# A graph layer with top-p attention on one core: work moved off GpSimd in one stage, a shorter sort on exponentials in the next

## Chip, cores and metric

The kernel runs on one core of one Trainium2 chip. The metric is device time in microseconds (us) from start to end of the program. Engines are named as in the profile: PE (TensorE matmul), PEld (its weight load), DVE (VectorE), ACT (ScalarE), POOL (GpSimd) and SP (the engine that only issues DMAs).

## What is computed

Two layers over 3327 nodes with 256 features, all in float32. The first is a graph attention layer with a gated update. The second, which holds nearly all of the change, makes two steps; in each, every node attends to all nodes, and of its probabilities only the largest that together reach 0.9 are kept:

```python
q = X @ W1.T @ W2.T
k = X @ W3.T
probs = softmax(q @ k.T)
sp, idx = probs sorted downwards, and its order
keep_sorted = cumsum(sp) - sp < 0.9
A = probs * (that mask, put back in place)
A = A / max(A.sum(-1), 1e-12)
...
for n in range(2):
    A = top_p_attention(Xa)
    Xf = R @ Xf          # R: sparse adjacency + identity, rows scaled to 1
    Xa = A @ Xa
    Z = Z + Xf @ U1[n].T + Xa @ U2[n].T
h = X + Z
x = layernorm(X + (layernorm(h) * ln_g + ln_b))
```

## The kernel before

Rows are worked on in 26 tiles of 128 (the last has 127). The program has four stages.

**Layer 0** (0 to 396 us). `Layer0.run` overlaps up to seven tiles; `Layer0.tile` is a generator in which `to(k)` puts what follows into the k-th turn, and a new tile opens every 6 turns. Its row result x1 is normalized at line 1049.

**Step 0** (396 to 1010 us). `Layer1.parts_0` defines the parts of a tile by name, and the table `ORDER_0` (line 75) gives each a tick. A tile opens every 32 ticks (`EVERY0`), so parts of up to six tiles interleave; a tick modulo 32 tells where a part stands in the steady order. PE, ACT, DVE and POOL run strictly in the order written (`manual_schedule`). A tile's path: logits for all nodes (L1720, copied by ACT at L1723), the eight largest of each 208 by MAX8 (L1736), a sort of the 40 largest by five rounds of MAX8 and MATCH_REPLACE8 (L1754, L1756), the cut-off `limit` (L1424 to L1444), signs (L1448), the list of the nodes that any row needs (L1457 to L1527), five gathers of those nodes on POOL (`needed`, L1537), their logits again (`turned` L1575, `by_nodes` L1594, `weights` L1602, `kept` L1607), the product (`attention` L1613, `one_over` L1620, `xa` L1626), and `xa_u` (L1353), whose result `c_out` copies (L1647) and `c_add` adds to x1 on POOL (L1652). Beside it runs the sparse side: five gathers of neighbours on POOL (L648), membership masks (`member`, five comparisons a tile, L1321), `adj_1`, `adj_2` (L1328, L1333), `xf` (L1338), `xf_u` (L1353), `y_out` (L1365, L1370), and the additions `y_add` and `y_add2` on POOL (L1374, L1378). `bias` adds ln_b to x1 on POOL and stores it (L1894). `limit_parts` splits the limit into three bfloat16 numbers in five small POOL operations (L1550 to L1554).

**Step 1** (1010 to 1609 us). `run` works tile by tile. For tile i the 26 transposes of the masked probabilities (`turn`, L1941, copied by ACT at L1943) and the product (`times`, L1957) go in 7 groups; in slots after the groups, parts of tiles i+1 and i+2 are put in. PE, ACT and DVE keep the order written; POOL's order is chosen by the framework. DVE's order for one tile is: 16 of tile i+1's 20 MAX8 of 167 (L1736), the last eight (L1741), a sort of 72 by nine rounds (L1754, L1756), 4 MAX8 of tile i+2 (`EARLY_GROUPS`), the cumulated sum and cut-off (`list_3`, L1832 and `settle`), and in slot 5 `mask`: MATCH_REPLACE8 over 3335 elements of the logits (L1860), then a comparison and product over 3327 (L1846), which makes the tile that PE transposes next. Logits of tile i+2 are made in slots 0, 2, 4 and 6. The exponentials of tile i+1 stand in slots 1 and 2 (L1812).

**Ends** (1609 to 1821 us). Rows whose kept set is longer than the list are put aside during step 1 and done in three groups of 128 (`hard`). Should more remain, a slow program computes everything anew.

Two logits arrays `l` and two probability arrays `p` alternate between tiles. PSUM pools hold two buffers each.

Of the kernel before, what the change touches and what calls it, by code (L numbers as in the profile page):

```python
# [79 lines left out]
        (37, "sort_2"), (40, "exp1"), (42, "adj_1"), (43, "sort_3"), (45, "exp0 exp_list"), (47, "bias"),  # L80
        (49, "settle_1 settle_2"), (58, "sign1"), (59, "sign0 adj_2"), (69, "count"), (72, "xf"), (74, "any_row"),
        (75, "prefix"), (77, "places"), (79, "hot_l hot_h"), (80, "xf_turned"), (82, "hot_b"), (83, "xf_copy"), (88, "placed"), (91, "node"), (94, "xf_u"),
        (99, "told"), (101, "y_out"), (102, "limit_parts"), (107, "y_add"), (112, "y_add2"), (116, "limit_turned"), (118, "limit_row"), (122, "index"), (124, "needed0"), (127, "needed3"), (135, "needed1"),
        (141, "needed4"), (143, "needed2"), (145, "turned"), (148, "turned_copy"), (150, "by_nodes weights"),
        (160, "kept"), (163, "attention"), (167, "one_over"), (170, "xa"), (172, "qk0"), (175, "qk1 qk2"),
        (178, "xa_u"), (180, "qk3"), (184, "c_out"), (191, "c_add"),
# [5 lines left out]
LIST = (40, 72)  # L92
EARLY_GROUPS = [
    g for h in range(2) for g in range(-(-h * HALF // GROUP[1]), (h * HALF + LC) // GROUP[1])
]
# [454 lines left out]
class Shared:  # L550


    def __init__(self, tc, ctx, x, W1T, W2T, W3T):
# [16 lines left out]
        self.weights = W1T, W2T, W3T  # L570
        self.xt_of = {}
# [123 lines left out]
class Layer0:  # L695
# [187 lines left out]
    def tile(self, t):  # L883
# [166 lines left out]
        move_rows(nc.scalar, sh.x1_rows[t * P : t * P + r, :], x1, r)  # L1050
        yield from to(42)
# [123 lines left out]
class Layer1:  # L1175
    def __init__(self, sh, ctx, U1T, U2T, ln_g, ln_b, out):
# [19 lines left out]
        self.b = keep.tile([P, D], F32, name="ln_b")  # L1196
        nc.sync.dma_start(self.b, ln_b.partition_broadcast(P))
        self.xu = keep.tile([P, NT, D], F32, name="xu")
        self.power = keep.tile([P, 1], F32, name="power")
        nc.vector.memset(self.power, -0.5)  # L1200
        self.ident16 = keep.tile([P, P], BF16, name="ident16")
# [61 lines left out]
    def parts_0(self, t):  # L1263
# [49 lines left out]
        @part  # L1313
        def bias():
            self.x_and_bias(t)

        @part
        def member():
            v.m1 = work.tile([P, EB, P], F32, tag="m", name=f"m{tag}")
            for b in range(EB):  # L1320
                nc.vector.tensor_scalar(v.m1[:, b, :], sh.col1, sh.erow[:, t, b : b + 1], None, ALU.is_equal)  # L1321
            nc.sync.dma_start(self.members[t], v.m1)
# [39 lines left out]
        @part  # L1362
        def y_out():
            v.y = work.tile([P, STEPS, D], F32, tag="xt", name=f"y{tag}", bufs=3)
            nc.scalar.activation(  # L1365
                v.y[:r].rearrange("p s d -> p (s d)"), v.py[:r], AF.Copy, scale=sh.rinv[:r, t : t + 1]
            )
            move_rows(nc.sync, sh.y_rows[t * P : t * P + r, :], v.y[:r, 1, :], r)
            v.own = work.tile([P, D], F32, tag="xf2", name=f"own{tag}")
            nc.scalar.activation(v.own[:r], v.y[:r, 1, :], AF.Copy, scale=sh.rinv[:r, t : t + 1])  # L1370

        @part
        def y_add():
            nc.gpsimd.tensor_tensor(sh.x1[:r, t, :], sh.x1[:r, t, :], v.y[:r, 0, :], ALU.add)  # L1374

        @part
        def y_add2():
            nc.gpsimd.tensor_tensor(sh.x1[:r, t, :], sh.x1[:r, t, :], v.own[:r], ALU.add)  # L1378
# [168 lines left out]
        def limit_parts():  # L1547
            v.three = self.st.tile([P, 3], BF16, tag="three", name=f"three{tag}", bufs=4)
            left = small("lleft", f"lleft{tag}")
            nc.gpsimd.tensor_copy(v.three[:r, 0:1], v.limit[:r])  # L1550
# [265 lines left out]
    def list_2(self, i):  # L1816
        for _ in self.items[i].sort:
            pass
# [637 lines left out]
```

## Time and profile before

| what | us |
|---|---|
| median of 3 runs (1827.29 to 1838.53) | 1833.26 |
| the profiled execution, its own time | 1823.47 |
| its span, first to last instruction | 1821.3 |
| layer 0 | 396.0 |
| step 0, full part (460 to 903) | 443.0 |
| step 1, steady part (1010.84 to 1491.00) | 480.2 |
| step 1, last tiles (1491 to 1609) | 118.0 |
| ends | 212.3 |

The stages were cut by the windows view at the first mask of step 1 (1010.84), and at its last regular and its last mask (1491.00 and about 1609). In a timeline line the columns are start, duration, engine, source line, operation, output and inputs with their shapes, count, and in brackets the idle time before it with what ended it. In the windows view a line is a stretch: its length, then busy time and instruction count of PE, PEld, DVE, ACT, POOL, then the granted clock of PE (1.00 is full), the share of DMA and GB/s.

### The profile page before, as it was taken

The numbers are of one execution on the slowest core, as the hardware profiler recorded it, in microseconds if no ns is written. First come the engines' busy times: TensorE is split into PE (matmuls) and PEld (weight loads), VectorE is DVE, ScalarE is ACT, GpSimd is POOL, SyncE is SP. The second block draws the span as 40 slices with busy tenths as digits, with TensorE's granted clock in tenths as the row PEclk, the third lists the DMA queues.
The fourth block names the chain that finished last, engine by engine and source line by source line (L and its number), as shares of the span: only waits on it lengthen the run. The fifth ranks groups of instructions, "written<-read, shape, count | busy, mean of one in ns | idle before, by whom it ended". The sixth has DMA issues, their size and how long they took to land.

```text
span 1821.3 us, 27585 instructions
## 1 busy us (share of the span) xinstructions
PE 1468.1 (81%) x7865; PEld 978.0 (54%) x7865; DVE 1432.0 (79%) x4680; ACT 1070.6 (59%) x2494; POOL 1156.2 (63%) x1962
## 2 busy tenths in 40 slices
PE   6399999977888888888887799999999987973333
PEld 5255555544544555545553577666667765652332
DVE  5788887448877888888841999999999996787793
ACT  3366666746766777777652456666666654666511
POOL 1577777625766777777653477777777776565311
PEclk9799999977889999999996899999999998995666
DMA  8877773323333333334332122222222212100000
GB/s 276 296 255 234 232 226 100 84 83 97 98 101 106 107 100 107 106 111 114 101 90 61 42 56 65 61 61 60 60 61 59 60 49 62 40 15 24 3 3 4
DMA packets 98686, 176.20 MB, mean 97 GB/s; under 512 B 25970, under 2 KB 61041, under 8 KB 98524
## 3 DMA queue, kind: packets, MB, share of 16 engines
q0 software_dynamic: 26480, 74.24, 16.0%
q1 hardware_dynamic: 53790, 83.24, 13.9%
q10 hardware_dynamic: 18254, 16.86, 2.8%
q8 instruction: 64, 1.05, 0.2%
q14 instruction: 98, 0.80, 0.1%
HBM read 137.17 MB, written 37.21 MB: 96 GB/s over the span
## 4 chain that ended last, share of the span: by engine, by line
PE 29%; POOL 22%; DVE 19%; ACT 15%; issue 11%; DMA 4%; POOLq 0%; ACTq 0%; SPq 0%; DVEq 0%
POOL g L648 10%; PE pav L1957 6%; DVE array L1860 5%; PE pl L1720 3%; POOL g L1537 3%; DVE array L1846 2%; DMA g<-x1k,uidx 2%; DVE p L1846 2%; ACT at L1943 2%; ACT array L1812 2%; PE pc L1353 2%; ACT p L1812 2%; PE pt L1941 2%; PE pav L1613 2%; PE pavh L1957 2%
## 5 line engine op out<-in xcount | busy, mean ns | idle before, releaser
L1957 PE MATMUL pav<-xu,at 128*128 128x256 f32 (+2 forms) x1352 | 334.1, 392 | 25.3 <-ACT at L1943 25.1
L1957 PEld LDWEIGHTS pav<-xu,at 128*128 128x128 f32 (+2 forms) x1352 | 247.7, 192 | 106.8 <-ACT at L1943 46.1
L1736 DVE MAX8 cand<-array 128x8 f32<-128x167 f32 (+5 forms) x921 | 243.7, 335 | 25.2 <-ACT array L1723 25.2
L1723 ACT COPY array<-pl 128x416 f32<-128x416 f32 (+3 forms) x402 | 182.4, 505 | 131.2 <-PE pl L1720 130.6
L1720 PE MATMUL pl<-kT,qT 64*128 64x416 f32 (+3 forms) x804 | 213.7, 573 | 19.5 <-ACT array L1723 14.6
L648 POOL DMA_INDIRECT g<-whx,edge x130 | 141.8, 1090 | 46.8 <-issue 36.1
L648 POOL DMA_INDIRECT g<-y_rows,edge x130 | 137.0, 1054 | 46.3 <-issue 30.5
L648 POOL DMA_INDIRECT g<-x_rows,edge x130 | 136.1, 1047 | 43.5 <-issue 34.8
L1537 POOL DMA_INDIRECT g<-x1k,uidx x130 | 137.7, 1060 | 37.9 <-issue 34.1
L1943 ACT COPY at<-pt 128x512 f32<-128x512 f32 (+2 forms) x182 | 93.4, 542 | 114.3 <-PE pt L1941 114.2
L1720 PEld LDWEIGHTS pl<-kT,qT 64*128 64x128 f32 (+1 forms) x804 | 73.0, 190 | 95.3 <-issue 49.8
L1754 DVE MAX8 lst<-cand 128x8 f32<-128x160 f32 (+3 forms) x364 | 113.4, 311 | 8.1
L867 DVE FIND_INDEX8 at<-ones,array 128x8 uint32<-128x840 f32 (+1 forms) x104 | 105.5, 1027 | 0.0
L1860 DVE MATCH_REPLACE8 array<-gone,array 128x3335 f32<-128x3335 f32 (+1 forms) x26 | 94.0, 3617 | 0.0
L1756 DVE MATCH_REPLACE8 cand<-lst,cand 128x160 f32<-128x160 f32 (+3 forms) x312 | 92.8, 297 | 0.0
L1992 POOL TENSOR_TENSOR h<-h,xb 128x256 f32<-128x256 f32 (+1 forms) x26 | 87.5, 3364 | 2.0
L1613 PE MATMUL pav<-g,w 128*128 128x257 f32 (+1 forms) x260 | 66.7, 405 | 16.6 <-ACT y L1365 13.2
L1884 PE MATMUL pxf<-g,m 128*128 128x256 f32 (+1 forms) x260 | 68.5, 414 | 3.7 <-DVE base L2027 3.7
L1613 PEld LDWEIGHTS pav<-g,w 128*128 128x128 f32 (+1 forms) x260 | 49.5, 198 | 39.9 <-ACT y L1365 28.8
L1652 POOL TENSOR_TENSOR x<-x,c 128x256 f32<-128x256 f32 (+1 forms) x26 | 22.0, 846 | 76.7 <-ACT c L1647 76.7
L1884 PEld LDWEIGHTS pxf<-g,m 128*128 128x128 f32 (+1 forms) x260 | 50.9, 204 | 36.3 <-issue 25.2
L988 PE MATMUL acc<-g,m 128*128 128x259 f32 (+1 forms) x260 | 64.1, 393 | 6.7 <-ACT m L984 6.7
(547 smaller groups left out, 3781.0 us busy)
## 6 DMA issues: line engine op xcount, KB each, us to landing
array<-in_adj_dram SPq DMA_DIRECT2D x23, 1248.0 KB
array<-in_adj_dram SPq DMA_DIRECT2D x23, 415.5 KB
members<-m SPq DMA_DIRECT2D x26, 320.0 KB
m<-members SPq DMA_DIRECT2D x26, 320.0 KB
whx<-table ACTq DMA_DIRECT2D x25, 129.5 KB
x_rows<-x ACTq DMA_DIRECT2D x25, 128.0 KB
x1k<-x ACTq DMA_DIRECT2D x25, 128.0 KB
xb_rows<-xb SPq DMA_DIRECT2D x25, 128.0 KB
```

Source lines behind the costliest of these rows:

```text
L648: self.nc.gpsimd.indirect_dma_start(out=dst[:, b, :], out_offset=None, in_=table[:, :], in_offset=bass.IndirectOffsetOnAxis(ap=self.edge[: ...
L867: nc.vector.max_index(at[:r, g, :], self.ones8[:r], ad[:r, g, :])
L1537: nc.gpsimd.indirect_dma_start(out=v.g2[:, b, :], out_offset=None, in_=sh.x1k[:, :], in_offset=bass.IndirectOffsetOnAxis(ap=v.idx[:, b : b ...
L1613: nc.tensor.matmul(v.acc[:r, : D + 1], v.w[:, b, :r], v.g2[:, b, : D + 1], start=(b == 0), stop=(b == UB - 1))
L1720: nc.tensor.matmul(pl[:r, :w], q[on], self.sh.kT[on, n, s : s + w], start=True, stop=True)
L1723: nc.scalar.copy(l[:r, h * HALF + s : h * HALF + s + w], pl[:r, :w])
L1736: self.nc.vector.max(cand[:r, g * 8 : g * 8 + 8], src[:r, g * group : min(N, (g + 1) * group)])
L1754: nc.vector.max(lst[:r, k : k + 8], cand[:r])
L1860: nc.vector.match_replace(rev, gone[:r], rev, -BIG)
L1884: nc.tensor.matmul(acc[:r, :D], v.m[:, b, :r], v.g[:, b, :], start=(b == 0), stop=(b == EB - 1))
L1943: nc.scalar.copy(at[:, :full, :r], pt[:, :full, :r])
L1957: nc.tensor.matmul(v.acc[: v.r, :D], at[:k, j - 4 * g, : v.r], V[:k, j, :], start=(j == 0), stop=(j == NT - 1))
```

## The change

In step 0, `y_add` and `c_add` go from POOL to DVE, which reads the products from PSUM; the copies in `y_out` and `c_out` that fed POOL go away; `limit_parts` goes to ACT; ln_b is added in layer 0 instead of in `bias`; the five comparisons of `member` become one; `ORDER_0` is laid out anew. In step 1, the largest logit comes from the candidates (`highest`), the exponentials are made a tile earlier, and exponentials instead of logits are sorted: all candidates at or above a bound are summed at once, if that sum is tested to lie under the threshold, and the next 40 are sorted in five rounds. Ties and mask work on `p` alone. The slots change: the logits of tile i+2 in slots 0 to 3, their MAX8 in slots 1 to 4, `mask` of tile i+1 in slot 4 after them.

```diff
 ORDER_0, ticks (before -> after):
-  (59, "adj_2") (72, "xf") (80, "xf_turned") (101, "y_out") (107, "y_add") (112, "y_add2") (102, "limit_parts")
-  (145, "turned") (163, "attention") (170, "xa") (178, "xa_u") (184, "c_out") (191, "c_add")
+  (48, "adj_2") (60, "xf") (66, "xf_turned") (101, "y_out") (103, "y_add") (105, "limit_parts")
+  (148, "turned") (164, "attention") (173, "xa") (181, "xa_u") (187, "c_out") (190, "c_add")
-LIST = (40, 72)
+LIST = (40, 40)
...
 # Layer0.tile, after x1 is made at turn 41
+        xb = self.work.tile([P, D], F32, tag="n", name=f"xb{t}")
+        nc.gpsimd.tensor_tensor(xb[:r], x1, sh.b[:r], ALU.add)
+        move_rows(nc.sync, sh.xb_rows[t * P : t * P + r, :], xb[:r], r)
...
 # parts_0
-            for b in range(EB):
-                nc.vector.tensor_scalar(v.m1[:, b, :], sh.col1, sh.erow[:, t, b : b + 1], None, ALU.is_equal)
+            nc.vector.tensor_tensor(v.m1, sh.col1 (broadcast), sh.erow[:, t, :] (broadcast), ALU.is_equal)
-            nc.gpsimd.tensor_tensor(sh.x1[:r, t, :], sh.x1[:r, t, :], v.y[:r, 0, :], ALU.add)
-            nc.gpsimd.tensor_tensor(sh.x1[:r, t, :], sh.x1[:r, t, :], v.own[:r], ALU.add)
+            for s, scale in enumerate((sh.rinv, self.rinv2)):
+                nc.vector.scalar_tensor_tensor(
+                    x1, v.py[:r, s * D : (s + 1) * D], scale[:r, t : t + 1], x1, ALU.mult, ALU.add
+                )
-            nc.gpsimd.tensor_tensor(sh.x1[:r, t, :], sh.x1[:r, t, :], v.c[:r], ALU.add)
+            nc.vector.tensor_tensor(sh.x1[:r, t, :], sh.x1[:r, t, :], v.pc2[:r, :D], ALU.add)
...
+    def list_1(self, i):
+        nc.vector.tensor_scalar(v.thr2[:r], v.sums[:r, 0:1], v.sums[:r, 1:2], 2.0 * TOP_P, ALU.add, ALU.mult)
+        nc.vector.tensor_reduce(high[:r], self.ranks(ec, r)[:, :, SKIP], AX.X, ALU.max)
+        v.last = self.last_eights(ec, r, tag)
+        nc.vector.scalar_tensor_tensor(v.cand[:r], ec[:r], high[:r], ec[:r], ALU.is_ge, ALU.mult, accum_out=above[:r])
+        nc.vector.scalar_tensor_tensor(over[:r], above[:r], 2.0, v.thr2[:r], ALU.mult, ALU.is_ge)
+        nc.vector.scalar_tensor_tensor(top[:r], over[:r], 2.0, high[:r], ALU.mult, ALU.max)
+        nc.vector.scalar_tensor_tensor(v.cand[:r], ec[:r], top[:r], ec[:r], ALU.is_lt, ALU.mult)
+        nc.vector.scalar_tensor_tensor(v.e[:r, 0:1], over[:r], 0.5, above[:r], ALU.is_lt, ALU.mult)
+        for _ in self.sort(v.cand, r, LIST[1], tag, v.lst):
+            pass
...
 # mask
-        self.drop(v.l[:r], v.d, v.t, r, 0, tag)
+        self.drop(v.p[:r], v.d, v.t, r, 0, tag)
-            v.p[:r], v.l[:r, :N], v.t[:r], v.p[:r], ALU.is_ge, ALU.mult, accum_out=sA[:r]
+            v.p[:r], v.p[:r], v.t[:r], v.p[:r], ALU.is_ge, ALU.mult, accum_out=sA[:r]
...
 # run, step 1
+                for k, pair in enumerate(pairs):
+                    slot(k, self.some_logits, i + 2, pair)
                 if i + 1 < total:
                     self.list_1(i + 1)
-                    slot(1, self.exp, i + 1, 0)
-                    slot(1, self.list_2, i + 1)
-                    slot(2, self.exp, i + 1, 1)
-                    slot(2, self.exp_list, i + 1)
+                    slot(0, self.list_2, i + 1)
+                for k, pair in enumerate(pairs):
+                    slot(k + 1, self.largest, i + 2, pair)
                 if i + 2 < total:
-                    slot(2, self.some_eights, i + 2, EARLY_GROUPS)
+                    slot(4, self.highest, i + 2)
+                    slot(5, self.exp_candidates, i + 2)
+                    slot(5, self.exp, i + 2, 0)
+                    slot(6, self.exp, i + 2, 1)
                 if i + 1 < total:
                     slot(3, self.put_aside_2, i)
-                    slot(3, self.list_3, i + 1)
-                    slot(5, self.mask, i + 1)
+                    slot(4, self.mask, i + 1)
                     slot(6, self.put_aside_1, i + 1)
...
-                for k, pair in enumerate(pairs):
-                    slot(2 * k, self.some_logits, i + 2, pair)
```

In the new `list_2` stand the cumulated sum and `settle` of the former `list_3`, now 40 wide. `largest(i, pair)` issues the MAX8 of those groups of 167 whose columns have all been copied: four after each of the first two pairs of chunks, six after the third, six after the fourth. At the handover, `first_1` makes the MAX8 of both first tiles of step 1 instead of one, and the exponentials of both follow. The three last groups (`hard`) keep a list of 72 (`HARD_LIST`).

## The prediction

> **What bounds the kernel now.** I read the page first, then the stages in the windows view, then one regular period of each large stage in windows and timeline. The page's first lines say that no engine is full over the whole:
>
> ```profile
> PE 1468.1 (81%) x7865; PEld 978.0 (54%) x7865; DVE 1432.0 (79%) x4680; ACT 1070.6 (59%) x2494; POOL 1156.2 (63%) x1962
> ```
>
> The averages hide two loops with different limits. Windows of step 0 (length, then busy PE, PEld, DVE, ACT, POOL, then the clock), one line for a tile at reduced clock, one at full clock:
>
> ```profile
> 690.00:711.80 21.80, 19.01 (x128) 11.07 (x127) 17.55 (x70) 15.26 (x32) 15.49 (x21) 0.92 0.37 103
> 752.71:773.11 20.40, 17.55 (x127) 10.44 (x126) 17.63 (x70) 15.24 (x33) 15.53 (x21) 1.00 0.39 111
> ```
>
> Here nobody is at 100%. The once-a-tile index instruction (L1532) starts at 460.17 and 21 tiles later at 902.95: 21.1 us a tile on average. What links the tiles is in the timeline of the second window:
>
> ```profile
> 750.36 0.16 DVE L1620 TENSOR_SCALAR rA<-pav 128x1 f32<-128x1 f32 x1 [2.01 <-PE pav L1613]
> ...
> 754.88 1.00 POOL L1537 DMA_INDIRECT g<-x1k,uidx  x1 [0.31 <-issue]
> ...
> 757.82 0.30 PE L1575 MATMUL pk<-ident,g 128*64 128x128 f32 x1 [1.43 <-DMA g<-x1k,uidx]
> ...
> 763.99 0.73 POOL L1652 TENSOR_TENSOR x<-x,c 128x256 f32<-128x256 f32 x1 [1.51 <-ACT c L1647]
> ```
>
> A ring: the last gather leaves POOL at 755.88, its data reach PE at 757.82, PE and ACT make c, POOL waits 1.51 us for c, adds it, and only then issues the gathers of the next tile. POOL idles 1.5 us, PE 1.4, DVE 2.0; each waits for the other. Outside that wait POOL is occupied for 18.9 of 20.4 us, since each of ten gathers takes 1.0 plus 0.3 of issue.
>
> Step 1, one period, and the loop inside it (chunk copies and the mask):
>
> ```profile
> 1238.45:1261.42 22.97, 21.58 (x107) 16.03 (x107) 21.62 (x64) 14.40 (x34) 17.22 (x29) 1.00 0.21 60
> ```
>
> ```profile
> 1238.53 3.62 DVE L1860 MATCH_REPLACE8 array<-gone,array 128x3335 f32<-128x3335 f32 x1
> ...
> 1242.18 4.17 DVE L1846 SCALAR_TENSOR_TENSOR array<-array,t,array 128x3327 f32<-128x3327 f32 x1
> ...
> 1242.95 3.99 POOL L1992 TENSOR_TENSOR h<-h,xb 128x256 f32<-128x256 f32 x1
> ...
> 1246.50 1.06 PE L1941 MATMUL pt<-ident,array 128*128 128x128 f32 x8 [0.62 <-DVE array L1846]
> ...
> 1247.07 3.81 DVE L1736 MAX8 cand<-array 128x8 f32<-128x167 f32 x16
> ...
> 1247.81 1.99 PE L1957 MATMUL pav<-xu,at 128*128 128x256 f32 x8 [0.24 <-ACT at L1943]
> ...
> 1250.17 0.97 PE L1720 MATMUL pl<-kT,qT 64*128 64x416 f32 x4
> ...
> 1251.17 0.92 ACT L1723 COPY array<-pl 128x416 f32<-128x416 f32 x2 [0.31 <-PE pl L1720]
> ```
>
> DVE has no idle but 0.45 us for the list's exponentials; after one tile's mask it starts at once on the next tile's MAX8, all of whose logits are there. DVE is the bound, PE (21.6) close behind. Masks start at 1010.84 and, 21 tiles later, at 1491.00: 22.87 us each.
>
> [...] the POOL addition above takes 3.99 us beside the two-input L1846, where the same shape takes 0.73 (L1991) elsewhere. [...] Here a window of 4 us with 2.20 us of PE work (692 to 696) is followed by one at 0.70 of the clock, while gaps near 1 us in other tiles leave it at 1.00.
>
> **Step 0, part by part.** *POOL* loses L1374, L1378, L1652, L1894 (0.75 + 0.75 + 0.85 + 0.77, means of the groups) and the five limit operations (0.25 apart, 1.3): 4.4 us, from 18.9 to 14.5; and nothing on it waits for c any more, so the ring is open. *DVE* gains two PSUM additions for y and one for c. Nearest row: DVE L1029 and L1338, 256 wide from PSUM, 0.42 and 0.41; together 1.25. `member`: five L1321 take 1.1; [...] (an estimate; the 640-wide L1607 takes 0.95): minus 0.3. DVE without its wait is 20.4 - 2.0 = 18.4; plus 0.95 is 19.4. Bounds: 18.8 if the small operations that POOL slows (L1490 to L1493, means 0.35 to 0.61 where the shortest are 0.18) speed up, 20.5 if the new order makes DVE wait again. *ACT* loses L1370 (0.51), L1647 (0.36), half of L1365 (0.2), gains five operations of about 0.2: zero, and it is 15.3 busy of 20. *PE* has the same work, 17.6. New period 19.7, DVE's, with 0.3 for waits; 21 x (21.1 - 19.7) = 29, with the ramps **-31 us** (-13 to -48).
>
> **Layer 0.** 26 additions of 0.77 and their stores are moved here. POOL is 7.8 busy of 10 us a tile, PE 10.0 (window 337.47 to 347.50), so 0.77 fits, but POOL now waits in order for ACT's x1 (L1049) and behind it stand a later tile's gathers; on SP the stores stand between the adjacency loads. **+3 us** (0 to +10).
>
> **Step 1: work.** DVE loses four rounds of sort, start to start 0.78: 3.1; the wait for the list 0.45, a memset 0.06, about 0.3 from 40 instead of 72 columns. It gains a reduction (0.19), two operations of 160 with one accumulator read (0.33 + 0.33 + 0.08; nearest row L1756, 0.31) and four tiny ones at 0.23: 1.85. Net -2.1: 20.9 us. If that set the pace, PE's 21.6 would be next.
>
> **Step 1: order.** But it does not. On DVE, `mask` of tile i+1 now stands behind `largest` of the last chunks and `highest` of tile i+2, and those chunks are in slot 3 of tile i, behind PE work that needs the mask of tile i. From mask to mask, with the durations above:
>
> - mask end to first transpose 0.14; transposes to first product 1.31 (1246.50 to 1247.81);
> - three groups of product 1.83, transposes 0.53, chunk 0.90 (1247.81, 1249.64, 1250.17, 1251.07): 3 x 3.26 = 9.78; then 1.83 + 0.53 to the fourth chunk: 13.6 in all;
> - chunk start to first copy's end 1.5 (copies start 1.0 after it, 0.46 each); six MAX8 at 0.24, last one full, 1.5 (the second copy is hidden under the first three); reduction 0.25; the two `gone` operations 0.53;
> - MATCH_REPLACE8 with its load 3.71; L1846 3.69 alone (1014.57) to 4.17 beside POOL's addition.
>
> Sum 13.6 + 11.2 to 11.65 = **24.8 to 25.3**, 25.1. DVE waits for chunks about 4 us in it, PE for the mask: after the fourth chunk PE has only 0.9 + 1.9 + 0.3 + 2.7 + 2.4 = 8.2 us of work against 11.5, a hole of 3 us. Before, that path had slack: chunks in slot 6, MAX8 after the mask. The hole may cost clock: a first group at low clock took 3.43 instead of 1.99 (1019.71), with its transposes 1.6 more. I take a fifth of the tiles, 0.3: 25.4 (24.8 to 26.7). 21 x (25.4 - 22.87) = **+53 us** (+40 to +80).
>
> **Handover and end.** Before, 9.3 us pass from last MAX8 (1001.5) to mask. Now: six more MAX8 1.5, `highest` 0.3, candidates' exponentials 0.4, two halves 1.9 each, `list_1` 5.5, cut-off 1.6, 0.5: 13.6. **+4**. The last tiles (1491 to 1609) hold a wait of PE for POOL's flag, 10.5 us before L2005; the flag's cut-off now comes earlier: **-4** (-14 to +8). The ends are unchanged: a list of 72 as before. Loading ln_b earlier and the single `rinv2` operation: under 1 us.
>
> **Sum.** -31 + 3 + 53 + 4 - 4 = **+25**. On the profiled execution, 1823.5 + 25 = 1848.5; it lies 9.8 below the median of the runs, 1833.3, to which I add the same 25: **1858**.
>
> **Rivals.**
> - *The loop does not close*: if the fourth chunk's way to the mask is hidden (the chunk reaches DVE before DVE is through with its other work), step 1 runs at PE's 21.6 to 21.8: 21 x -1.15 = -24, total -52, about 1781. For it: DVE and PE loads are both below 22. Against: the order is written out and strict. It decides at a period of 24.2: there the loss of 21 x 1.33 equals the 28 gained elsewhere. Chance 0.20; this one ends on the other side.
> - *The clock falls in every tile*, 25.1 + 1.6 = 26.7: +80, total +52, 1885. For it: the hole of 3 us; against: [...] work around it is dense. 0.14.
> - *Step 0 gains nothing*, as three more operations on DVE's strict order wait for PE while POOL's release is worth nothing: +56, 1889. For it: DVE is the next bound by 1 us only. 0.07.
> - *The bound test does not hold*, too many rows are put aside, and the slow program runs: thousands of us. No view speaks for it; 0.01.
> - The forecast: 0.58, its own range 1832 to 1884.
>
> Faster by over 1% (below 1815): the first rival and a corner of the forecast, 0.21. Within 1% (to 1851.6), about what a measurement can tell: 0.22 of the forecast and 0.02, 0.24. Slower: 0.55. The range: 1786 leaves about 0.12 below, 1898 about 0.06 above.
>
> **What will show it.** Right: in step 1, mask starts 25 us apart, PE's first transpose waiting about 3 us for DVE L1846's successor, DVE's last MAX8 waiting for ACT, DVE busy below 21. Wrong: a wait under 1 us there and a period below 23. In step 0: a period of 19.5 to 20, no POOL wait for c, DVE's wait for L1620's successor below 0.5; wrong if the period stays at 20.4 or more. In layer 0: POOL waiting for ACT x1 before the new addition, stage end near 399. At the handover: the first mask some 13 to 14 us after the last MAX8.

## The result and the profile after

The changed kernel takes 2042.11 us (median of 4 runs, 2030.28 to 2050.05) against 1830.38 for the kernel before beside it: ratio 1.1144, 95% interval 1.1074 to 1.1213. It is slower by a ninth, where the prediction had +25 us (1858), and outside the predicted range.

The page's line of engines. Every engine but DVE and POOL has more busy time than before, PE by 143 us for the same 7865 instructions:

```profile
PE 1611.3 (79%) x7865; PEld 1054.9 (52%) x7865; DVE 1396.9 (68%) x4499; ACT 1081.6 (53%) x2569; POOL 1039.8 (51%) x1754
```

Cut at the same marks as before (the index instruction L1532 of step 0, the masks of step 1), the profiled executions (own times 1823.47 and 2050.05, spans 1821.3 and 2048.3) differ by 227.0 us:

| stage | before | after | predicted | measured |
|---|---|---|---|---|
| layer 0, to the first index instruction | 438.7 | 451.2 | +3 | +12.5 |
| step 0, 25 intervals of that instruction | 522.6 (20.90 each) | 637.8 (25.51 each) | -31 | +115.2 |
| last index instruction to first mask | 49.6 | 59.9 | +4 | +10.3 |
| step 1, 21 steady tiles | 480.2 | 573.0 | +53 | +92.8 |
| last tiles and ends | 330.2 | 326.3 | -4 | -3.9 |

Windows of the changed kernel: one regular tile of step 0, one of step 1 (length; busy PE, PEld, DVE, ACT, POOL; clock):

```profile
839.65:864.41 24.76, 20.77 (x131) 11.66 (x130) 17.05 (x69) 15.64 (x36) 10.65 (x12) 0.93 0.30 85
1366.96:1394.27 27.31, 24.06 (x107) 17.81 (x107) 19.67 (x59) 14.74 (x34) 16.55 (x28) 0.88 0.17 51
```

In step 0 DVE and POOL are busy for less than the prediction said (17.05 and 10.65), PE for more (20.77 instead of 17.6), and yet a tile takes 24.8: no engine is full, a longer chain is the bound. PE's surplus goes with its clock. The same windows over the full part of step 0, for the kernel before, the changed kernel, and the changed kernel with the old ticks (an experiment below):

```profile
460.00:903.00 443.00, 383.17 (x2641) 224.72 (x2641) 368.15 (x1448) 319.98 (x649) 324.12 (x421) 0.96 0.38 105
460.00:990.00 530.00, 437.11 (x2526) 246.64 (x2523) 341.60 (x1364) 307.01 (x677) 215.61 (x224) 0.85 0.29 80
460.00:903.00 443.00, 380.12 (x2696) 227.39 (x2693) 366.33 (x1467) 333.09 (x728) 238.17 (x238) 0.99 0.40 102
```

The clock of PE is 0.85 instead of 0.96 and 0.99, and PE is busy for about 21 us a tile instead of 18 (busy time over length, times the interval between tiles). No run takes this apart from the waits that come with it.

In step 1 DVE lost 2.0 us of work a tile and the tile became 4.3 longer; PE's work grew by 2.5 because its clock is 0.88.

Where step 0 waits, by the waits view of the stretch 460 to 990:

```profile
POOL uidx L1532 <- DMA back<-ulist: 234.6, 20, 16.7
DVE x L1650 <- ACT xu L1646: 136.6, 19, 9.5
ACT w L1602 <- PE plt L1594: 71.6, 18, 5.2
```

The wait that stood at this place before, POOL's for c (44.2 us in step 0), is gone. DVE now waits three times as long for the other half of the same product, and POOL waits for the list of nodes. The timeline of one period and of the start of the next:

```profile
864.41 0.19 POOL L1532 TENSOR_SCALAR uidx<-back 128x5 uint32<-128x5 f32 x1 [10.87 <-DMA back<-ulist]
...
871.98 1.98 PE L1357 MATMUL pc<-u,xtq 128*128 128x512 f32 x4
...
875.60 0.37 PE L1594 MATMUL plt<-qT,kg 64*128 64x128 f32 x1
...
876.55 0.27 PE L1594 MATMUL plt<-qT,kg 64*128 64x128 f32 x1 [0.57 <-issue]
...
880.33 3.78 PE L1357 MATMUL py<-u,xft 128*128 128x512 f32 x4
...
880.43 0.76 ACT L1602 ACTIVATE w<-plt 128x384 f32<-128x384 f32 x2 [5.08 <-PE plt L1594]
...
881.08 1.68 ACT L1448 ACTIVATE array<-array,limit 128x1663 bf16<-128x1663 f32 x1
...
882.65 0.37 ACT L1646 COPY xu<-pc 128x256 f32<-128x256 f32 x1
...
883.06 0.42 DVE L1650 TENSOR_TENSOR x<-x,pc 128x256 f32<-128x256 f32 x1 [7.18 <-ACT xu L1646]
...
885.38 0.81 DVE L1607 SCALAR_TENSOR_TENSOR w<-w 128x640 f32<-128x640 f32 x1
...
886.11 0.15 DVE L1524 TENSOR_TENSOR node<-node,pu 32x20 f32<-32x20 f32 x1
...
886.34 2.41 PE L1613 MATMUL pav<-g,w 128*128 128x257 f32 x10 [0.17 <-DVE node L1524]
...
889.53 0.19 POOL L1532 TENSOR_SCALAR uidx<-back 128x5 uint32<-128x5 f32 x1 [11.42 <-DMA back<-ulist]
...
902.16 0.37 PE L1594 MATMUL plt<-qT,kg 64*128 64x128 f32 x1
```

The product pc is complete at 873.96. Its copy `c_out` (L1646) could run then, but on ACT it stands behind the next tile's `weights` (L1602), which wait until 880.43 for `by_nodes` (L1594), and behind a sign half of 1.68 us. (By the ticks, `c_out` stood behind the next tile's `weights` before, too, at 184 against 150 + 32 = 182; at 187 the sign half of 58 + 128 = 186 stands ahead of it as well.) `c_add` on DVE (L1650) reads the same PSUM tile and is ordered after that copy, so it starts at 883.06, 9.1 us after its data. Behind it on DVE stand `kept` (L1607), which ends at 886.19, and `node`. `attention` on PE starts 0.15 us after `kept`, and PE then goes through its written order, with no wait above 1.58 us, to the next `by_nodes` at 902.16. From `by_nodes` to `by_nodes` that ring is 26.6 us. It is read from the trace; the experiments below test parts of it. Two things in it are not waits: `by_nodes` itself takes 4.8 us in this period, where it takes 0.96 on average in the kernel before (gaps marked "issue" between its matmuls, see "PE's slow stretches"), and a product on PE runs at reduced clock (3.78 us at 880.33 for work that took 1.98 at 871.98).

POOL's long wait is not part of this ring. `node` feeds the list, which goes through memory (3.3 us), and POOL's index instruction waits for it; but for its 60 transposes of gathered nodes (L1575) from 460 to 990 PE shows no wait put down to such a gather, where it waited 29.5 us for them from 460 to 903 before. The gathers after 864.41 are the ones that the transposes from 895.48 on read, and the last of them left POOL at 878.12.

Over the 26 tiles, DVE's idle time before `c_add` that is put down to the copy `c_out` comes to 189.3 us.

The timeline of a period of step 1, mask to mask:

```profile
1366.96 3.61 DVE L1874 MATCH_REPLACE8 array<-gone,array 128x3327 f32<-128x3327 f32 x1
...
1368.65 0.74 POOL L1999 TENSOR_TENSOR h<-h,xb 128x256 f32<-128x256 f32 x1
...
1370.61 3.69 DVE L1860 SCALAR_TENSOR_TENSOR array<-array,t 128x3327 f32<-128x3327 f32 x1
...
1371.48 3.82 POOL L650 DMA_INDIRECT g<-y_rows,edge  x1 [2.10 <-PE pxf L1898]
...
1374.41 1.57 PEld L1948 LDWEIGHTS pt<-ident,array 128*128 128x128 f32 x8 [3.62 <-issue]
1374.45 1.94 PE L1948 MATMUL pt<-ident,array 128*128 128x128 f32 x8 [3.25 <-DVE array L1860]
...
1376.21 3.78 PE L1964 MATMUL pav<-xu,at 128*128 128x256 f32 x8
...
1381.62 1.99 PE L1964 MATMUL pav<-xu,at 128*128 128x256 f32 x8
...
1390.50 0.97 PE L1712 MATMUL pl<-kT,qT 64*128 64x416 f32 x4
...
1392.04 1.49 DVE L1728 MAX8 cand<-array 128x8 f32<-128x167 f32 x6 [1.70 <-ACT array L1715]
...
1394.27 3.61 DVE L1874 MATCH_REPLACE8 p<-gone,p 128x3327 f32<-128x3327 f32 x1
```

This is the predicted loop: PE waits 3.25 us for the mask, DVE waits for the fourth chunk, the mask follows. Its three legs are mask 7.34 (1366.96 to 1374.30), mask end to fourth chunk 16.20 (to 1390.50), chunk to next mask 3.77: 27.31. The first product after the hole takes 3.78 instead of 1.99.

### The profile page after: what moved, and what is told of

It is laid out like the page before. It is cut to its first block, busy times and chain, and to the rows that moved or that the text cites. A ratio compares the mean times of both kernels' runs of the same rounds, so it can differ in the third digit from the quotient of the medians.

```text
span 2048.3 us, 27176 instructions
## 1 busy us (share of the span) xinstructions
PE 1611.3 (79%) x7865; PEld 1054.9 (52%) x7865; DVE 1396.9 (68%) x4499; ACT 1081.6 (53%) x2569; POOL 1039.8 (51%) x1754
## 5 line engine op out<-in xcount | busy, mean ns | idle before, releaser
L1964 PE MATMUL pav<-xu,at 128*128 128x256 f32 (+2 forms) x1352 | 374.4, 426 | 23.8 <-ACT at L1950 23.8
L1964 PEld LDWEIGHTS pav<-xu,at 128*128 128x128 f32 (+2 forms) x1352 | 270.2, 210 | 126.2 <-issue 45.9
L650 POOL DMA_INDIRECT g<-y_rows,edge x130 | 186.7, 1436 | 81.7 <-PE pxf L1898 44.6
L1532 POOL TENSOR_SCALAR uidx<-back 128x5 uint32<-128x5 f32 x26 | 5.0, 192 | 295.0 <-DMA back<-ulist 294.9
L1650 DVE TENSOR_TENSOR x<-x,pc 128x256 f32<-128x256 f32 (+1 forms) x26 | 10.9, 421 | 189.3 <-ACT xu L1646 189.3
L1613 PE MATMUL pav<-g,w 128*128 128x257 f32 (+1 forms) x260 | 81.1, 471 | 54.3 <-DVE node L1524 40.4
L1948 PE MATMUL pt<-ident,array 128*128 128x128 f32 x338 | 65.1, 333 | 39.6 <-DVE array L1860 39.6
L1948 PE MATMUL pt<-ident,p 128*128 128x128 f32 (+1 forms) x338 | 63.2, 326 | 34.0 <-DVE p L1860 34.0
L1948 PEld LDWEIGHTS pt<-ident,array 128*128 128x128 f32 x338 | 54.5, 178 | 53.5 <-issue 47.1
L1357 PE MATMUL py<-u,xft 128*128 128x512 f32 (+1 forms) x104 | 77.6, 887 | 1.3 <-issue 1.3
L1602 ACT ACTIVATE w<-plt 128x384 f32<-128x384 f32 (+3 forms) x52 | 19.9, 434 | 109.4 <-PE plt L1594 88.1
L1948 PEld LDWEIGHTS pt<-ident,p 128*128 128x128 f32 (+1 forms) x338 | 53.1, 174 | 46.9 <-issue 38.4
```

The source lines that it names most:

```text
L650: self.nc.gpsimd.indirect_dma_start(out=dst[:, b, :], out_offset=None, in_=table[:, :], in_offset=bass.IndirectOffsetOnAxis(ap=self.edge[: ...
L1613: nc.tensor.matmul(v.acc[:r, : D + 1], v.w[:, b, :r], v.g2[:, b, : D + 1], start=(b == 0), stop=(b == UB - 1))
L1948: nc.tensor.transpose(pt[: rows(j), j - j0, :r], v.p[:r, cols(j)], self.ident[:r, :r])
L1964: nc.tensor.matmul(v.acc[: v.r, :D], at[:k, j - 4 * g, : v.r], V[:k, j, :], start=(j == 0), stop=(j == NT - 1))
```

## The experiments

Two theories stood for step 0: **A**, the moved operations cost (DVE, PE or POOL are worse off with them); **B**, the new ticks cost (where parts stand in the order). For step 1 a **loop** theory (the order closes it, the hole lowers the clock) stood against **work**. "Spacing" is the mean interval of the index instruction in step 0 (20.9 before, 25.5 after); it is of one profiled execution each time. After each measured time stand its ratio to the kernel before and the 95% interval.

### Which half costs what

**Step 0 as before, the rest as after** (table and operations put back; ln_b stays in layer 0).

> The kernel after with step 0 as before (order of ticks, c_add, y_add, y_add2 and limit_parts on POOL, five comparisons in member); the addition of ln_b stays in layer 0 and step 1 stays as after. Theory (the two halves of the change lose separately, step 0 about 138 us up to the first mask, step 1 about 93 in its steady part): index instructions 21.1 us apart, first mask at 1005 to 1020, masks 27.3 us apart as in the kernel after, total 1895 to 1920. Rival (the addition in layer 0, or the earlier candidates and exponentials at the end of step 0, cost a part of it): first mask above 1030, total above 1930.

Measured: 1931.59, ratio 1.053 (1.049 to 1.057). Spacing 21.2, masks 27.3 apart, first index instruction at 454.9. Step 1 and layer 0 together account for 5.3 of the 11.4 per cent. First mask (1035.92) and total are on the rival's side of its limits (1030 and 1930): the addition in layer 0 costs a part. From the last index instruction to the first mask it is 51.9, 2.3 more than before.

**New table, old operations.**

> The kernel after, with the new table ORDER_0 kept, but with the operations of step 0 as before: c_add and y_add on POOL behind ACT's copies, limit_parts on POOL, five comparisons in member (y_add2 stands in y_add's tick). Theory A (the moved operations lengthen step 0: DVE gets work that waits for PE, ACT gets limit_parts): index instructions 20.4 to 22.5 us apart, total 1935 to 1980. Theory B (the new table itself makes the ring: the list, the attention and xa_u stand later against by_nodes, and PE's long waits come from there): they stay 24.5 to 26 us apart, total 2025 to 2060.

Measured: 2014.27 (one run; 1822.06 before on that chip), spacing 24.6, first mask 1115.39. The table alone does most of the harm; B holds for the spacing, and the total is a little below what it gave. The old operations show the same queue, with POOL in DVE's place (its pc was complete at 791.37):

```profile
793.57 0.76 ACT L1604 ACTIVATE w<-plt 128x384 f32<-128x384 f32 x2 [3.71 <-PE plt L1596]
...
794.22 1.68 ACT L1450 ACTIVATE array<-array,limit 128x1663 bf16<-128x1663 f32 x1
...
795.79 0.37 ACT L1649 COPY c<-pc 128x256 f32<-128x256 f32 x1
...
796.25 0.72 POOL L1654 TENSOR_TENSOR x<-x,c 128x256 f32<-128x256 f32 x1 [6.77 <-ACT c L1649]
```

Here the ring does go through POOL: its gathers stand behind this addition, and PE waits for them (460 to 890), as it did before and does not in the changed kernel:

```profile
PE pk L1577 <- DMA g<-x1k,uidx: 49.6, 17, 3.7
```

**New operations, old ticks** (the changed kernel with only the table put back; `c_out` and `c_add` ahead of `weights`, since the old places do not fit the PSUM buffers):

```diff
- (48, "adj_2") (60, "xf") (66, "xf_turned") (69, "xf_copy") (103, "y_add") (105, "limit_parts")
- (148, "turned") (153, "by_nodes weights") (164, "attention") (173, "xa") (181, "xa_u") (187, "c_out") (190, "c_add")
+ (59, "adj_2") (72, "xf") (80, "xf_turned") (83, "xf_copy") (102, "y_add limit_parts")
+ (145, "turned") (150, "by_nodes weights") (163, "attention") (170, "xa") (178, "xa_u") (181, "c_out") (182, "c_add")
```

> The kernel after with only the ticks of step 0 put back (old ones, save y_add at 102, c_out at 181, c_add at 182); operations, layer 0 and step 1 as after. Theory (the table costs what step 0 lost): first mask at 960 to 1010 instead of 1149, masks 27.3 us apart as in the kernel after, total 1865 to 1910. Rival (both moves together): first mask above 1060, total above 1950.

Measured: 1911.26, 1.0441 (1.0399 to 1.0483). Spacing 20.4, first mask 1009.47 instead of 1149.00, masks still 27.3 apart. The total is 1.3 us above the range expected of the theory, the first mask within it. The ticks cost 7 of the 11.4 per cent, the place of `c_out` among them.

### What in the table

**c_add before c_out** (ticks of the two exchanged, and `y_add` before `y_out`).

> The kernel after, with only the written order changed in step 0: c_add (DVE) stands before c_out (ACT), and y_add before y_out, so that the additions on DVE wait for PE alone; in the kernel after both read the same PSUM tile after ACT's copy and wait for ACT. Theory (DVE stands about 6 us a tile behind ACT's queue, and the list, its round trip to DRAM and the gathers come late for that): DVE's wait for ACT at L1650 (189 us in the kernel after) falls below 20 us, POOL's wait for the list's rows (295 us) below 120, the index instructions stand 19.5 to 21.5 us apart instead of 25.9, total 1900 to 1930. Rival (the new order of ticks, or the load on DVE, makes the loop): spacing stays at 24.5 or more, total above 2005.

Measured: 2043.84, 1.1171 (1.1105 to 1.1238); spacing 25.7. DVE's wait for ACT is gone, but `c_out` now stands still later, and the next `attention`, which needs its PSUM buffer, waits for it (14.6 us of PE, 24.5 of its weight loads, from 460 to 990). The wait moved; nothing was gained, and spacing and total are what the rival gave. It was no clean test, since it moved `c_out` the wrong way.

**c_out ahead of weights** (`c_out` 187 to 184, `c_add` 190 to 185).

> The kernel after, with two ticks changed in the table of step 0: c_out from 187 to 184 and c_add from 190 to 185, so that on ACT the copy of xa_u's product stands before weights and sign1 of other tiles, and the addition on DVE right behind it; nothing else. Theory (the new table puts c_out behind weights and sign1 on ACT, so that c_add on DVE, and all that DVE has behind it, and the release of the product's PSUM buffer for attention, come some 4 to 6 us late in every tile): DVE's wait for ACT before c_add falls from 189 us to under 60, index instructions 20.5 to 22.5 us apart, total 1945 to 1985. Rival (the ring is elsewhere in the new table, for instance in turned, by_nodes and placed on PE): they stay above 24, total above 2010.

Measured: 1991.61 (one run; 1833.07 before), spacing 23.8, first mask 1097.32 (51.7 earlier). The place of `c_out` (with `c_add` right behind it) is worth 1.7 of the 4.6 us a tile. That lies between what theory and rival gave: the queue on ACT is a part of the loss.

**Mixed tables**: new operations, new ticks for the sparse path, old ones for the dense path, ln_b in step 0, step 1 with opened slots. They differ in `c_out` / `c_add`: 184 / 185, then 181 / 182, then 183 / 181 (addition first). The logits stand in slots 0, 0, 1, 2 in the first two (the text of the first says 0, 0, 1, 1) and in 0, 1, 1, 2 in the third.

> Step 0 with the new operations (additions on DVE, limit_parts on ACT, one comparison) but with the dense path's ticks as before (turned 145 to xa_u 178, c_out 184, c_add 185); the sparse path's ticks as after; ln_b added in step 0 on POOL; step 1 as after with its logits in slots 0, 0, 1, 1. Theory (the moved operations are harmless, the new ticks of the dense path are what costs): POOL has no wait for c, index instructions 19.5 to 20.6 us apart (20.9 before with its starts and ends), first mask at 985 to 1012, total 1800 to 1830. Rival (the operations on DVE and ACT cost too): 21.5 or more apart, first mask above 1025, total above 1845.

> As the kernel with mixed ticks (dense path's ticks as before the change, sparse path's as after, new operations, ln_b added in step 0), but c_out at tick 181 and c_add at 182 instead of 184 and 185, so that on ACT the copy stands before weights; logits of step 1 in slots 0, 0, 1, 2. Theory (in the mixed kernel the ring runs through weights on ACT, c_out behind it, c_add on DVE and the PSUM buffer that xf_u waits for; with c_out ahead of weights it is open, and the moved operations are harmless): DVE's wait for ACT before c_add under 25 us, index instructions 20 to 21.5 us apart, first mask at 995 to 1020; step 1 at 22.5 to 23.1 us a tile; total 1800 to 1830. Rival (the moved operations, or PE's slow stretches, cost in any table): above 22.5 apart, first mask above 1035, total above 1845.

> The same with c_add at 181 and c_out at 183, so that the addition on DVE waits for PE alone and the copy on ACT for the addition; logits of step 1 in slots 0, 1, 1, 2. Theory: step 0 as in the kernel with c_out at 181 within 0.5 us a tile, step 1 within 0.4 us a tile of the one with slots 0, 0, 1, 2, total within 15 us of it. Rival (the copy, now behind the addition on DVE, is late for ACT's weights and for attention): 1 us a tile or more above it.

Measured: 1896.54, 1.0329 (1.0285 to 1.0373); 1878.84, 1.0232 (1.0179 to 1.0286), spacing 22.8; 1884.75, 1.0271 (1.0222 to 1.0321), 22.9. The first two missed what was expected of them: none comes back to the kernel before. The third kept within what was expected. At 184 `c_out` is again behind `weights` of the old dense ticks, and its wait returns (77.5 us of DVE from 520 to 950, in a profiled run of 1917.11, the longest of the four; the other three are 1885.32 to 1900.93); ahead of them, the order of the two hardly matters. The 2 us left (22.8 against 20.9) lie with the sparse ticks or with the operations.

**Sparse ticks alone** (kernel before with all moves and old ticks, then `adj_2`, `xf`, `xf_turned`, `xf_copy` at the new ones).

> As the kernel before with all the moves under old ticks, but with the sparse path's ticks of the change: adj_2 48 for 59, xf 60 for 72, xf_turned 66 for 80, xf_copy 69 for 83. Theory (the mixed kernels at 22.4 us a tile differ from the old table in these ticks alone): 22 to 23 us a tile, by_nodes or placed above 1.3 us on average, total 1815 to 1860. Rival (they are harmless): within 0.5 us a tile of the kernel without them.

Measured: 1843.24 (one run; 1834.54 before); spacing 21.9 against 21.2 without. That is 0.7 us a tile, less than the theory gave and more than the rival did, and not clear of the noise: 22 runs of the kernel without took 1821.69 to 1843.26.

### Which of the moves pays

All from the kernel before, with its table, step 1 untouched. *c*: `c_add` to DVE, `c_out` 184 to 181, `c_add` 191 to 182. *y*: `y_add` and `y_add2` as one part on DVE at 102. *limit*: `limit_parts` on ACT and the single comparison.

```diff
-  (178, "xa_u"), (180, "qk3"), (184, "c_out"), (191, "c_add"),
+  (178, "xa_u"), (180, "qk3"), (181, "c_out"), (182, "c_add"),
-  nc.gpsimd.tensor_tensor(sh.x1[:r, t, :], sh.x1[:r, t, :], v.c[:r], ALU.add)
+  nc.vector.tensor_tensor(sh.x1[:r, t, :], sh.x1[:r, t, :], v.pc2[:r, :D], ALU.add)
```

> The kernel before, with the complement: only c_add is moved to DVE (c_out at tick 181, c_add at 182), everything else, y_add, y_add2 and limit_parts on POOL among it, as before. Theory: POOL no longer waits for c and runs ahead; PE's slow stretches appear (by_nodes or placed above 1.3 us on average), index instructions 21.5 to 23 us apart, total 1855 to 1890. Rival (opening POOL's ring helps, as the prediction had it): 19.5 to 20.3 apart, total 1805 to 1825.

> The kernel before, with part of the change in step 0: y_add on DVE (both products, from PSUM, at tick 102), limit_parts on ACT, one comparison in member; c_add stays on POOL behind ACT's copy, the table is otherwise the old one, step 1 and layer 0 as before. Theory (these operations are harmless; PE's slow stretches in by_nodes and placed come only with c_add off POOL, when POOL runs ahead and waits for the list alone): index instructions 19.7 to 20.9 us apart, by_nodes on PE 0.9 to 1.0 us on average, total 1805 to 1838. Rival (the additions on DVE or limit_parts on ACT bring the loss): above 21.5 apart, by_nodes or placed above 1.4 us on average, total above 1850.

> The kernel before with all the moves of step 0 (c_add and y_add on DVE, limit_parts on ACT, one comparison in member) under the old ticks, save y_add at 102, c_out at 181 and c_add at 182; ln_b in step 0, step 1 and layer 0 as before. Theory (the new ticks are at fault): 18.8 to 20.0 us a tile, first mask at 945 to 985, by_nodes 0.93 us, total 1750 to 1795. Rival (both moves together, POOL nearly free, bring the loss and PE's slow stretches): 21.5 or more a tile, total above 1830.

> c_add and y_add on DVE under the old ticks, limit_parts on POOL and member with five comparisons as before. If limit_parts on ACT is what tips it: 19.2 to 20.0 us a tile, placed 1.0 us, total 1765 to 1795. If not: 20.8 or more a tile, total 1820 or more.

> The kernel before with c_add on DVE (c_out 181, c_add 182), limit_parts on ACT and one comparison in member; y_add and y_add2 stay on POOL. If y_add on DVE is what spoils the pair (it frees the PSUM buffer late for attention): 19.2 to 19.8 us a tile, total 1770 to 1795. If any second move does: 20.5 or more, total 1800 or more.

| moved | median | ratio (interval) | spacing | first mask |
|---|---|---|---|---|
| c | 1779.34 | 0.9773 (0.9733 to 0.9813) | 19.5 | 970.02 |
| y, limit | 1791.62 | 0.9827 (0.9793 to 0.9862) | 20.0 | 982.37 |
| c, y, limit | 1835.76 | 1.0008 (0.9992 to 1.0024) | 21.2 | 1016.33 |
| c, y | 1812.08 | 0.9959 (0.9937 to 0.9982) | 20.7 | 998.16 |
| c, limit | 1766.45 | 0.9718 (0.9699 to 0.9738) | 18.9 | 946.44 |

*c* and *c, y, limit* missed what was expected of them: the first was to lose and gains, the second was to gain and does not. With *c* alone POOL no longer waits for c, as the ring of the prediction has it: spacing 19.5, and the first mask 41 us earlier (the prediction had 19.7 and 31 us, for all moves together). But *c* moves `c_out` ahead of `weights` as well, and `c_out` at 181 with `c_add` left on POOL was not run, so that the two are not told apart. POOL's longest wait in that kernel (470 to 900):

```profile
POOL uidx L1532 <- DMA back<-ulist: 36.3, 22, 1.9
```

*c* pays alone, and so does *y, limit*; *c* with *y* gives most of it back. A part of the reason is in the trace of the pair *c, y*: `y_add` on DVE releases the PSUM buffer that `attention` waits for, 44.6 us in 21 tiles:

```profile
699.76 0.48 DVE L1374 SCALAR_TENSOR_TENSOR x<-py,rinv,x 128x256 f32<-128x256 f32 x1
...
700.39 2.41 PE L1611 MATMUL pav<-g,w 128*128 128x257 f32 x10 [2.37 <-DVE x L1374]
```

With `y_add` left on POOL, which reads ACT's copy, that buffer is ACT's to release. *c, limit*, without *y*, then did better than was expected if *y* is what spoils the pair. A window of it, one tile:

```profile
690.00:708.90 18.90, 17.69 (x128) 10.64 (x127) 16.58 (x67) 16.10 (x36) 14.27 (x15) 1.00 0.42 118
```

*y, limit* without *c* has the same wait (33.7 us) and still pays, so the wait is not the whole of it; what else the pair does was not taken apart. All moves together give 21.2 here and 20.4 in the changed kernel with the old ticks, which differs in layer 0 and step 1 (and so in where ln_b is added); neither is the 19.7 of the prediction. *c, limit* is the fastest version run; it beats both kernels. It was not joined with a new step 1, since no order of that tried here was faster than the old.

**PE's slow stretches.** With both moves, some tiles show `placed` (L1513) or `by_nodes` with gaps of 0.5 us ahead of single matmuls, here in *c, y, limit*:

```profile
609.25 0.22 PE L1513 MATMUL pu<-p 128*64 128x40 bf16 x2 [0.22 <-issue]
...
609.98 0.18 PE L1513 MATMUL pu<-p 128*64 128x40 bf16 x1 [0.50 <-issue]
...
610.70 0.19 PE L1513 MATMUL pu<-p 128*64 128x40 bf16 x1 [0.55 <-issue]
```

A rival theory had it that they are the loss. The kernel *c, y, limit* got idle POOL additions (two of 256 columns, five of one) at the places where POOL had lost work.

> The kernel with both moves under the old ticks, and on POOL, where y_add, y_add2 and limit_parts stood, two additions of 256 columns and five of one column that nobody needs (the output is unchanged). Theory POOL's timing (gathers that run ahead meet PE's work): placed on PE below 1.1 us on average instead of 1.45, 19.4 to 20.3 us a tile instead of 21.2, total 1775 to 1810. Theory load (DVE and ACT): 21 us a tile or more, total 1830 or more.

Measured: 1818.88, 0.9966 (0.9945 to 0.9986); spacing 21.0. The stretches vanish, the tile gains 0.2; both theories had one half right. They come with POOL's timing, and they are not the loss in that kernel. In the changed kernel `by_nodes` takes 2.56 us on average instead of 0.96 (460 to 903); with the old operations in the new table it takes 0.97, and that kernel still has 24.6. So most of the table's loss comes without them; what they add to it in the changed kernel, where `by_nodes` lies on the ring, was not tried. What makes the gaps stays open.

### Step 1

**Logits earlier** (changed kernel, all four pairs of chunks in slots 0 and 1; the loop theory's cure).

```diff
-                    slot(k, self.some_logits, i + 2, pair)
+                    slot(k // 2, self.some_logits, i + 2, pair)
```

> The kernel after with one edit in step 1: the four pairs of chunks of logits stand in slots 0, 0, 1, 1 instead of 0 to 3; the MAX8 and the mask keep their slots. Theory (from mask to mask a loop runs through PE's third product group, the fourth pair of chunks, MAX8 and mask; the clock falls only in the hole which that loop makes): the fourth pair comes some 5 to 8 us sooner, DVE and PE loads of 21 to 22 us set the pace, masks 21.6 to 22.5 us apart, clock above 0.97, total 1925 to 1945. Rival (the masks are held by something else, such as the exponentials on ACT or the sort): 24 us or more apart, total above 1970.

Measured: 1948.91, 1.0625 (1.0573 to 1.0677). Masks 23.33 apart, clock 1.00. The loop theory holds: opened, it gives 4 us a tile, though 23.3 and not the 21.6 to 22.5 expected. One of the four runs took 4794.79 us and does not count in the ratio (without it the median is 1947.04); in the same series one of seven runs of the kernel before took 3537.59. Why is not known.

**A filler in PE's hole** (changed kernel; six matmuls between tiles, their result unused).

```diff
+            for _ in range(6):
+                self.nc.tensor.matmul(pf[:, :D], self.ident, self.xu[:, 0, :], start=True, stop=True)
```

> The kernel after with six more matmuls of 128x256 in each tile of step 1, put between one tile's product and the next tile's transposes, where PE stands idle for 3.25 us; their result goes to a PSUM tile that nobody reads, and the output is unchanged. Theory (the idle time lowers PE's clock in every tile, and slow PE work lies on the loop from mask to mask for 2 to 2.6 us): PE works more and the masks come 24.9 to 25.5 us apart instead of 27.3, total 1985 to 2005. Rival (the slow first groups have another reason, contention with DVE's mask or ACT's copies): spacing 27.0 or more, total 2030 or more.

Measured: 1996.49, 1.0883 (1.0803 to 1.0963). The window of a tile (12 matmuls more than above, as the profile counts the six as 12), and the timeline of such a place:

```profile
1361.05:1385.74 24.69, 23.80 (x119) 17.92 (x119) 19.61 (x59) 14.65 (x34) 16.57 (x28) 1.00 0.18 57
```

```profile
1365.12 2.75 PE L2241 MATMUL fill<-xu,ident 128*128 128x256 f32 x12
...
1368.53 1.06 PE L1949 MATMUL pt<-ident,p 128*128 128x128 f32 x8 [0.66 <-DVE p L1861]
...
1369.83 1.99 PE L1965 MATMUL pav<-xu,at 128*128 128x256 f32 x8 [0.24 <-ACT at L1951]
```

More work on PE makes the tile 2.6 us shorter: the loop stays (24.69), only the clock is held at 1.00. That separates the two: the order costs 24.7 - 22.9 = 1.8 us a tile, the clock 2.6.

**Step 0 wholly as before, step 1 with opened slots** (ln_b back in step 0; logits in slots 0, 0, 1, 2, not 0, 0, 1, 1 as the text of the expectation says).

> Step 0 wholly as before (table, operations, ln_b added in step 0 and not in layer 0), step 1 as after but with the four pairs of chunks of logits in slots 0, 0, 1 and 1 replaced by 0, 0, 1, 2's earlier form (0, 0, 1, 1), that is the loop taken apart. Theory (layer 0's addition costs about 10 to 15 us at the start of step 0, since the first index instruction stood at 438.7 us before and at 446.6 to 454.9 in the kernels with it): first index instruction at 437 to 441, first mask at 1012 to 1022, masks 23.3 us apart, total 1830 to 1850. Rival (the late start has another reason): first index instruction above 445, total above 1850.

Measured: 1830.61, 1.0053 (1.0032 to 1.0074); first index instruction at 438.16, masks 23.39 apart, as was expected. Even opened, step 1 as changed is 0.4 us a tile slower than before. Against the kernel with step 0 as before but ln_b in layer 0 (454.9), the first index instruction is 17 us earlier: that is what the addition in layer 0 costs there.

## Why the prediction was wrong

- **The failed step is "Step 0, part by part"**, its lines on ACT ("zero"), on PE ("the same work") and "New period 19.7, DVE's, with 0.3 for waits". It summed each engine's work and took the new ticks as neutral. Period 25.5 instead of 19.7, and the step's worst case was 20.5. The old ticks under the same operations (with `c_out` ahead of `weights`) give 20.4; the ticks cost 7 per cent, about 128 us of 1832. What was not traced is where `c_out` stands on ACT after the move (behind `weights` and a sign half), who reads the same PSUM tile, and what then queues behind `c_add` on DVE. PE does not have "the same work, 17.6" either: it is busy for about 21 us a tile, at a clock of 0.85. The bound "if the new order makes DVE wait again" named the right engine and gave the wait 0.8 us; it is 7. Of the 5.1 us a tile that the ticks cost (25.5 against 20.4), 1.7 are the place of `c_out`, and 0.7 at most is seen for the sparse ticks; the rest, with what the clock and PE's slow stretches add, was not taken apart.
- **The ring and its opening** were right as far as the runs show. POOL's wait for c did go; with the old ticks the move of `c_add` alone, with `c_out` three ticks earlier, gives 19.5 and -41 us. That 19.5 is near 19.7 is partly luck, since all moves under the old ticks give 20.4 to 21.2. In the changed kernel one ring was opened and another was closed through PE, ACT and DVE.
- **The sum of costs** that it used was good: `member` takes 0.816 us against 1.1 for the five operations, so its minus 0.3, the author's estimate, which no trace of before showed, held; `c_add` takes 0.42, as its nearest row. It was the order, not the work.
- **Layer 0**: +3 predicted, +12.5 in the ledger, the 17 above between two versions; outside its bound of +10. POOL waits 10.3 us for ACT's x1 there (300 to 460), as the step named, but that was priced too low; the rest was not traced.
- **Handover**: 2.3 more with the old step 0 (predicted 4). The other 8 us of the ledger belong to the new ticks' last tiles: with the old ticks under the new operations the stretch is 47.1.
- **Step 1, order**: the mechanism was right, with the hole predicted at 3 and measured at 3.25. The term mis-sized is the clock: 0.3 a tile, as a fifth of the tiles was assumed to be hit, the author's estimate. All are, at 2.6, which the filler shows. The leg from mask end to fourth chunk was 13.6 in the working and is 16.20; the legs around it fit (11.2 to 11.65 against 7.34 + 3.77 = 11.1). A tile is 2.6 - 0.4 - 0.3 = 1.9 us longer than forecast, 21 x 1.9 = 40: the distance from +53 to +92.8.
- **The rivals.** *The clock falls in every tile* was the right one for step 1, at 26.7 a tile (27.3 measured), but had 0.14, by the author's estimate; it was joined to a gain of step 0 that did not come. *Step 0 gains nothing* had the right doubt about DVE's strict order, but put the worst of it at no gain, where 115 us were lost. *The loop does not close* was priced at 21.6 to 21.8; the kernels with opened slots show 23.33 to 23.39, so its own price was too low as well. *The bound test does not hold* shows in none of the four runs of the changed kernel; the run of 4794.79 us above is not explained, but one of 3537.59 came without that test, in the kernel before.
- **Last tiles and ends**: -4 predicted, -3.9 measured.

## What to carry to other kernels

When an order is written by hand, follow the moved instruction on every engine's queue (what it stands behind, who reads the same buffer, what queues behind it) before adding up durations: in step 0 the work of POOL and DVE fell and a tile became 22 per cent longer. Test a new table of places apart from the moved operations; moves that pay apart can lose most of it together, here in part because one of them put a buffer's release on a queue that comes to it later. A hole of some 3 us in PE's work that returns in every tile has to be priced with the clock's fall in every tile: here 3.25 us of hole, a clock of 0.88 and 2.6 us a tile.

## What the hardware showed that was not expected

- The hole in step 1 is 3.25 us between matmuls (whose ends are modelled) and 3.62 between weight loads, and the clock falls after it in every steady tile (mean clock 0.87 from 1149 to 1722, first product 3.78 instead of 1.99); 2.75 us of idle matmuls in it keep 1.00. The window of the kernel before that the prediction showed goes further: its clock of 0.70 came after a stretch of 4 us with 2.20 us of PE work, in which no wait of PE was longer than 1.36 us. There the clock fell with no single gap as long as the hole. In step 1 the hole costs 2.6 us a tile.
- POOL's addition takes 0.74 us beside the mask's first operation (L1874), where it took 3.99 beside the second one of before. The second operation (L1860) takes 3.69 again, as it did before without POOL's addition beside it, and POOL is still slow beside it: in the five tiles from 1340 to 1480 the gather that started beside it took 3.82 to 3.83 us (1371.48 is one), the other four of each tile 0.99 to 1.03.
- Masks are 23.33 us apart with the logits in slots 0, 0, 1, 1 and 23.39 with 0, 0, 1, 2 and with 0, 1, 1, 2: the first arrangement that opens the loop is as good as the others. What sets this period was not tried.
